# A residual batch of per-sample matrix products: one small transfer more at the head of SyncE's queue, and another condition for the first store

## The chip, the core and the metric

The kernel runs on one core of a Trainium2 chip. A core has engines with instruction queues of their own: TensorE (PE, the matrix products), VectorE (DVE), ScalarE (ACT), GpSimd (POOL) and SyncE (SP). They agree with one another through semaphores: an instruction may wait until a semaphore has reached a number, and raise one when it is done. Transfers between the HBM and the on-chip memory (SBUF) are done by 16 DMA engines, which all queues share; an instruction on SyncE or ScalarE issues a transfer, and the transfer raises a semaphore by 16 once it has landed. Products land in PSUM, a memory of accumulators that VectorE reads.

The metric is the device time of one execution in microseconds. The profile shows one execution; its span reaches from the first to the last instruction and is a little shorter than the time.

## The reference

A batch of 128 samples, each a matrix of 128 channels by 1024 steps in float32. Each sample names one of 8 subjects, each subject has a 128 by 128 weight matrix, and the output is the sample plus the product with its subject's matrix.

```python
# x: (128, 128, 1024) f32; itok_B_0_7: (128,) int32 in 0..7; L0_cond_weights: (8, 128, 128) f32
w = weights[subjects]
out = jnp.einsum('bct,bcd->bdt', x, w)
x = x + out
```

Input and output are 67.1 MB each, so at least 134.2 MB cross between HBM and SBUF; the weights add 0.5 MB.

## The kernel before

**Tiles and slots.** The work is cut into `NT` = 32 units of `H * G` = 4 samples (2 MB). `x_all` holds 12 slots (`SLOTS`) of one unit each, side by side in SBUF; unit i uses slot i modulo 12. A unit has two halves (h = 0, 1) of two samples. The result of a unit is written over its input in the slot, and the store goes out from there.

**ScalarE issues the loads** (lines 200 to 204): 4 transfers of 512 KB for each unit, all in order. The first 12 units wait for nothing; from unit 12 on, the loads of a unit wait until the store of the unit 12 before, out of the same slot, has landed (`emptied`). So 48 loads can be issued at once.

**GpSimd** (206 to 211) only waits for loads to land and tells TensorE, by `s_ready`.

**VectorE** first clears `zeros` and a piece of `index`, waits for the subject list (line 194, semaphore `s_given`), clamps and wraps it in three small steps (195 to 199), waits for the weights, and copies the matrices of the first four samples from `w_all` into `ws`. Then a loop over the units (226): for each half it waits for the products, adds PSUM and the slot's half in one instruction of 128 x 2048 elements (`add`, line 174, which raises `s_added` by 1), and copies the two weight matrices for the same half of the next unit (`place`, line 153).

**TensorE** runs three idle products on `zeros` and then a loop over the units (231): for each half it waits for the weights (`s_go`) and the data (`s_ready`) and makes four products of 512 columns.

**SyncE** has the subject list as its first transfer (line 180, one piece of 512 bytes, `s_given`), then the weights (line 181, 1,024 pieces of 512 bytes, `s_wall`). Then come the stores (213 to 218). Ahead of all of them it waits until the loads of slot 7 have landed (line 213, `AHEAD` = 8); after that, each store waits for its unit's two additions (line 217: `s_added` at 2i + 2 for unit i). A unit's store is one transfer of 2 MB; the last unit goes in smaller parts, and its last sample on line 238.

What stands ahead of line 213 on SyncE are the two small transfers; what stands behind it are the stores alone.

Of the kernel before, what the change touches and what calls it, by code (L numbers as in the profile page):

```python
# [30 lines left out]
G = 2  # L31
H = 2
# [4 lines left out]

P_SLOTS = 2

AHEAD = 8  # L40

DMA = 16

# [29 lines left out]
def kernel(  # L73
# [7 lines left out]
    nc = tc.nc  # L81
    B, C, T = x.shape
    S, _, D = weights.shape
    NT = B // (G * H)

    def sbuf(name, *shape, dtype=F32):
        return ctx.enter_context(nc.sbuf_tensor(name, list(shape), dtype)).ap()
# [10 lines left out]
    w_all = sbuf("w_all", C, S, D)  # L98
    ws = [sbuf(f"w{i}", C, 1, D) for i in range(H * G)]
    zeros = sbuf("zeros", C, N)  # L100
    given, near, wrap = (sbuf(name, 1, B, dtype=I32) for name in ("given", "near", "wrap"))
    index = sbuf("index", 1, B + H * G, dtype=I32)
    ps = [
# [3 lines left out]
    s_given = tc.alloc_semaphore("s_given")  # L107
# [4 lines left out]
    s_added = tc.alloc_semaphore("s_added")  # L112
# [4 lines left out]
    s_slot = [tc.alloc_semaphore(f"s_slot{k}") for k in range(SLOTS)]  # L117
    s_head = tc.alloc_semaphore("s_head")

    def emptied(i):  # L120
        turns = i // SLOTS
        return DMA * (H * G + 1) * turns - (DMA * G if i >= SLOTS and i % SLOTS == 0 else 0)

    def load(engine, i, q):
        transfer(
            nc,
            engine,
            xs[i % SLOTS][:, q, :],
            x[i * H * G + q].rearrange("(a r) t -> a (r t)", r=ROWS),
        ).then_inc(s_head if i * H * G + q < G else s_slot[i % SLOTS], DMA)  # L130

    def store(i, q0, q1):
        b = i * H * G
        transfer(
            nc,
            nc.sync,
            out[b + q0 : b + q1].rearrange("g d t -> d g t"),
            xs[i % SLOTS][:, q0:q1, :].rearrange("d (o g) t -> d o (g t)", g=min(G, q1 - q0)),
        ).then_inc(s_slot[i % SLOTS], DMA)

    def subjects_of(i):
        _, subject = nc.values_load_multi_w_load_instructions(
            index[0:1, i] if isinstance(i, slice) else index[0:1, bass.ds(i * (H * G), H * G)],
            engines=[mybir.EngineType.DVE],
            min_val=0,
            max_val=S - 1,
            skip_runtime_bounds_check_because="the index is clamped on the chip above",
        )
        return subject

    def place(h, subject):
        for q in range(h * G, (h + 1) * G):
            copy = nc.vector.tensor_copy(ws[q], w_all[:, bass.ds(subject[q], 1), :])  # L153
        copy.then_inc(s_go, 1)

    def multiply(slot, h):
        nc.tensor.wait_ge(s_go, 1).then_inc(s_go, -1)
        nc.tensor.wait_ge(s_ready, 1).then_inc(s_ready, -1)  # L158
        for q in range(h * G, (h + 1) * G):
            for t in range(0, T, N):  # L160
                at = slot * (H * G * T) + (q * T + t)
                mm = nc.tensor.matmul(  # L162
                    ps[h][:, q % G, t : t + N],
                    ws[q][:, 0, :],
                    x_all[:, bass.ds(at, N)],
                    start=True,
                    stop=True,
                )
        mm.then_inc(s_product, 1)

    def add(slot, h):
        mine = x_all[:, bass.ds(slot * (H * G * T) + h * G * T, G * T)]
        nc.vector.wait_ge(s_product, 1).then_inc(s_product, -1)  # L173
        nc.vector.tensor_tensor(  # L174
            mine, ps[h].rearrange("d g t -> d (g t)"), mine, ALU.add
        ).then_inc(s_added, 1)

    with tc.tile_critical():  # L178

        nc.sync.dma_start(given, subjects.rearrange("(o b) -> o b", o=1)).then_inc(s_given, DMA)  # L180
        nc.sync.dma_start(w_all, weights.rearrange("s c d -> c s d")).then_inc(s_wall, DMA)

        nc.vector.memset(zeros, 0.0).then_inc(s_zeros, 1)  # L183
        nc.tensor.wait_ge(s_zeros, 1)
        for _ in range(IDLE):
            nc.tensor.matmul(  # L186
                ps[P_SLOTS - 1][:, G - 1, :N], zeros[:, :D], zeros, start=True, stop=True
            )

        nc.vector.memset(index[:, B:], 0).then_inc(s_index, 1)  # L193
        nc.vector.wait_ge(s_given, DMA)
        nc.vector.tensor_scalar(near, given, -S, S - 1, ALU.max, ALU.min).then_inc(s_index, 1)  # L195
        nc.vector.wait_ge(s_index, 2)
        nc.vector.tensor_scalar(wrap, near, 0, S, ALU.is_lt, ALU.mult).then_inc(s_index, 1)  # L197
        nc.vector.wait_ge(s_index, 3)
        nc.vector.tensor_tensor(index[:, :B], near, wrap, ALU.add).then_inc(s_index, 1)  # L199
        for i in range(NT):  # L200
            if i >= SLOTS:
                nc.scalar.wait_ge(s_slot[i % SLOTS], emptied(i))
            for q in range(H * G):
                load(nc.scalar, i, q)

        for i in range(NT):
            if i == 0:
                nc.gpsimd.wait_ge(s_head, DMA * G).then_inc(s_ready, 1)
                nc.gpsimd.wait_ge(s_slot[0], DMA * G).then_inc(s_ready, 1)
            else:  # L210
                nc.gpsimd.wait_ge(s_slot[i % SLOTS], emptied(i) + DMA * H * G).then_inc(s_ready, H)

        nc.sync.wait_ge(s_slot[AHEAD - 1], DMA * H * G)
        for i in range(NT):
            for h in range(H):
                if i == NT - 1 or h == H - 1:
                    nc.sync.wait_ge(s_added, i * H + h + 1)
                    store(i, h * G if i == NT - 1 else 0, (h + 1) * G - (i * H + h == NT * H - 1))


        nc.vector.wait_ge(s_index, 4)
        nc.vector.wait_ge(s_wall, DMA)
        subject = subjects_of(slice(0, H * G))
        for h in range(H):
            place(h, subject)
        with nc.vector.Fori(0, NT) as turn:  # L226
            subject = subjects_of(turn + 1)
            for h in range(H):
                add(turn % SLOTS, h)
                place(h, subject)  # L230
        with nc.tensor.Fori(0, NT) as turn:
            for h in range(H):
                multiply(turn % SLOTS, h)
# [39 lines left out]
```

## Time and profile before

| | |
|---|---|
| time, median of 3 runs | 323.64 us (323.44 to 323.72) |
| time of the profiled execution | 323.44 us |
| its span | 321.7 us |
| TensorE products busy | 244.1 us (76%) |
| VectorE busy | 165.7 us (52%) |
| bytes read from HBM, written to it | 67.63 MB, 67.11 MB |
| SyncE's queue (q1), share of the 16 DMA engines | 50.1% |
| ScalarE's queue (q10), share of the 16 DMA engines | 49.6% |
| loads: 128 of 512 KB, median from issue to landing | 10.7 us |
| 2 MB stores: 31, median from issue to landing | 54.8 us |
| weights: issue to landing | 5.1 us |

How to read the profile: the page cuts the span into 40 equal slices and gives each engine's busy share in tenths (9 is 90% or more). The row DMA is the mean busy share of the 16 DMA engines, and below it stands what they moved in GB/s. A transfer is cut into packets that the engines work off one by one; a share over 1 in a short stretch comes of packets that overlap or reach past it. In a timeline a line gives start, length, engine, source line, operation and tiles; "SPq" and "ACTq" are the issuing queues of SyncE and ScalarE, and "x48" merges 48 instructions. L59 is the line in the helper `transfer` where all loads and stores are made, so loads and stores are told apart by their tiles and queues.

### The profile page before, as it was taken

The page shows a single profiled execution, that of the slowest core. Times are in us where ns is not written, and L with a number is a line of the kernel's source. Part 1 is how long each engine was busy: PE and PEld are TensorE (multiplying, and loading weights), DVE is VectorE, ACT ScalarE, POOL GpSimd, SP SyncE. Part 2 cuts the span into 40 slices and gives each one's busy share as a digit, 9 for nine tenths or more (in the row PEclk, how much of TensorE's full clock was granted, in tenths as well). Part 3 has the DMA queues.
Part 4 walks back from the last instruction along what each step waited for, and adds up shares of the span by engine and source line. Part 5 has one row for each costly group of instructions (what it writes and reads, how often), then busy time and mean ns, then how long its engine had stood idle before and what let it go on. Part 6 is the DMA issues. An engine that isn't in the chain of part 4 may idle for free. (4 is left out here: it accounts for less than half of the span.)

```text
span 321.7 us, 2380 instructions
## 1 busy us (share of the span) xinstructions
PE 244.1 (76%) x518; PEld 101.0 (31%) x518; DVE 165.7 (52%) x202; POOL 0.2 (0%) x4
## 2 busy tenths in 40 slices
PE   5999999999999999959499684986959779300000
PEld 2434444443444444424143231432423234000000
DVE  2267776777677677736627465371754707500000
POOL 0000000000000000000000000000000000000000
PEclk9799999999999999979879999897998959755555
DMA  7999999999999999999999999999999999999997
GB/s 281 426 428 426 424 424 408 421 437 418 421 438 428 422 418 426 439 427 423 424 418 425 434 435 413 426 433 427 428 418 425 440 417 421 426 430 425 427 428 309
DMA packets 16051, 134.76 MB, mean 419 GB/s; under 512 B 2609, under 2 KB 3634, under 8 KB 3890
## 3 DMA queue, kind: packets, MB, share of 16 engines
q1 hardware_dynamic: 9906, 67.64, 50.1%
q10 hardware_dynamic: 6144, 67.12, 49.6%
q14 instruction: 1, 0.01, 0.0%
HBM read 67.63 MB, written 67.11 MB: 419 GB/s over the span
## 5 line engine op out<-in xcount | busy, mean ns | idle before, releaser
L162 PE MATMUL ps<-x_all,w 128*128 x512 | 239.6, 626 | 30.2 <-PEq L158 27.1
L174 DVE TENSOR_TENSOR x_all<-ps,x_all 128x2048 f32 x64 | 146.7, 2292 | 106.9 <-DVEq L173 106.9
L162 PEld LDWEIGHTS ps<-x_all,w 128*128 128x128 f32 x512 | 99.3, 199 | 170.5 <-issue 169.7
L153 DVE COPY w<-w_all 128x128 f32 x132 | 23.2, 219 | 4.3 <-DMA w_all<-in_L_cond_weights_dram 4.3
L186 PE MATMUL ps<-zeros 128*128 128x512 f32 x6 | 4.4, 897 | 1.7 <-DVE zeros L183 1.7
L186 PEld LDWEIGHTS ps<-zeros 128*128 128x128 f32 x6 | 1.7, 304 | 3.6 <-issue 1.9
L183 DVE MEMSET zeros<- 128x512 f32 x1 | 0.5, 485 | 1.0 <-SPq L178 1.0
L195 DVE TENSOR_SCALAR near<-given 1x128 int32<-1x128 int32 x1 | 0.2, 217 | 0.6 <-DMA given<-in_itok_B_dram 0.6
L199 DVE CUSTOM_DVE_ANT_0 index<-near,wrap 1x256 uint16<-1x256 uint16 x1 | 0.3, 280 | 0.0
L197 DVE TENSOR_SCALAR wrap<-near 1x128 int32<-1x128 int32 x1 | 0.2, 215 | 0.0
L260 POOL MEMSET const-bfloat16-1.0<- 128x1 bf16 x1 | 0.1, 101 | 0.0
L260 POOL MEMSET const-uint8-127<- 128x1 uint8 x1 | 0.1, 101 | 0.0
L260 POOL MEMSET const-float32-0.0<- 128x1 f32 x1 | 0.1, 98 | 0.2 <-issue 0.2
L260 POOL MEMSET const-float32-1.0<- 128x1 f32 x1 | 0.1, 98 | 0.0
L260 DVE BASE_LOAD x1 | 0.0, 21 | 0.1
L193 DVE MEMSET index<- 1x4 int32 x1 | 0.1, 62 | 0.0
## 6 DMA issues: line engine op xcount, KB each, us to landing
x_all<-in_x_dram ACTq DMA_DIRECT2D x128, 512.0 KB, 10.7
out_dram<-x_all SPq DMA_DIRECT2D x31, 2048.0 KB, 54.8
out_dram<-x_all SPq DMA_DIRECT2D x1, 1024.0 KB, 26.0
out_dram<-x_all SPq DMA_DIRECT2D x2, 512.0 KB, 21.0
w_all<-in_L_cond_weights_dram SPq DMA_DIRECT2D x1, 512.0 KB, 5.1
given<-in_itok_B_dram SPq DMA_DIRECT2D x1, 0.5 KB
```

The source lines that it names most:

```text
L153: copy = nc.vector.tensor_copy(ws[q], w_all[:, bass.ds(subject[q], 1), :])
L162: mm = nc.tensor.matmul(ps[h][:, q % G, t : t + N], ws[q][:, 0, :], x_all[:, bass.ds(at, N)], start=True, stop=True,)
L174: nc.vector.tensor_tensor(mine, ps[h].rearrange("d g t -> d (g t)"), mine, ALU.add).then_inc(s_added, 1)
L183: nc.vector.memset(zeros, 0.0).then_inc(s_zeros, 1)
L186: nc.tensor.matmul(ps[P_SLOTS - 1][:, G - 1, :N], zeros[:, :D], zeros, start=True, stop=True)
L193: nc.vector.memset(index[:, B:], 0).then_inc(s_index, 1)
L195: nc.vector.tensor_scalar(near, given, -S, S - 1, ALU.max, ALU.min).then_inc(s_index, 1)
L197: nc.vector.tensor_scalar(wrap, near, 0, S, ALU.is_lt, ALU.mult).then_inc(s_index, 1)
L199: nc.vector.tensor_tensor(index[:, :B], near, wrap, ALU.add).then_inc(s_index, 1)
L260: nc = _bacc.Bacc("TRN2", target_bir_lowering=False, num_devices=1)
```

## The change

`AHEAD` becomes 4, and the wait for slot 7's loads goes away. In its place the condition of the stores of units 0 to 3 is raised: each waits until both additions of unit 3 are done (`s_added` at 8). From unit 4 on the condition is the same as before. Besides, SyncE issues a transfer ahead of the subject list: 16 pieces of 512 bytes out of the first 16 channels of sample 0, into a new tile `opening` of 16 partitions that nothing reads. It raises the same semaphore as the subject list, so VectorE's first step waits for both (32 instead of 16).

```diff
-AHEAD = 8
+AHEAD = 4
...
+    opening = sbuf("opening", DMA, D)
...
+        nc.sync.dma_start(opening, x[0, :DMA, :D]).then_inc(s_given, DMA)
         nc.sync.dma_start(given, subjects.rearrange("(o b) -> o b", o=1)).then_inc(s_given, DMA)
         nc.sync.dma_start(w_all, weights.rearrange("s c d -> c s d")).then_inc(s_wall, DMA)
...
-        nc.vector.wait_ge(s_given, DMA)
+        nc.vector.wait_ge(s_given, DMA * 2)
...
-        nc.sync.wait_ge(s_slot[AHEAD - 1], DMA * H * G)
         for i in range(NT):
             for h in range(H):
                 if i == NT - 1 or h == H - 1:
-                    nc.sync.wait_ge(s_added, i * H + h + 1)
+                    nc.sync.wait_ge(s_added, max(i, AHEAD - 1) * H + h + 1)
                     store(i, h * G if i == NT - 1 else 0, (h + 1) * G - (i * H + h == NT * H - 1))
```

## The prediction

> **What bounds the kernel now.** I read the page first, for the busy tenths and the DMA rows, then the DMA share by stretches of the span, then the waits of SyncE's queue, and last the timelines of the issuing queues and of VectorE. From the page:
>
> ```profile
> span 321.7 us, 2380 instructions
> DMA  7999999999999999999999999999999999999997
> GB/s 281 426 428 426 424 424 408 421 437 418 421 438 428 422 418 426 439 427 423 424 418 425 434 435 413 426 433 427 428 418 425 440 417 421 426 430 425 427 428 309
> DMA packets 16051, 134.76 MB, mean 419 GB/s; under 512 B 2609, under 2 KB 3634, under 8 KB 3890
> ```
>
> The DMA engines are full in 38 of 40 slices. No compute engine is: TensorE and VectorE stop for good in slice 34, long before the end. The bytes are fixed, so the time is the bytes at the full rate, plus what is lost where the rate falls. The view by stretches shows where that is; its columns are microseconds, the length, each engine's busy time, granted clock, DMA share and GB/s:
>
> ```profile
> 0.00:2.30 2.30, 0.64 (x1) 0.50 (x2) 0.59 (x4) 0.20 (x4) 1.00 0.22 50
> 2.30:6.30 4.00, 3.79 (x6) 1.20 (x4) 0.63 (x3) 0.00 (x0) 1.00 0.99 344
> 6.30:48.00 41.70, 39.70 (x87) 16.68 (x88) 26.10 (x34) 0.00 (x0) 0.96 1.01 428
> 48.00:51.00 3.00, 3.00 (x9) 1.32 (x8) 1.83 (x2) 0.00 (x0) 1.00 0.95 344
> 51.00:280.00 229.00, 196.94 (x420) 81.34 (x418) 136.57 (x162) 0.00 (x0) 0.94 1.01 426
> 280.00:319.20 39.20, 0.00 (x0) 0.00 (x0) 0.00 (x0) 0.00 (x0) 0.50 1.01 425
> 319.20:320.40 1.20, 0.00 (x0) 0.00 (x0) 0.00 (x0) 0.00 (x0) 0.50 0.31 126
> 320.40:321.70 1.30, 0.00 (x0) 0.00 (x0) 0.00 (x0) 0.00 (x0) 0.50 0.00 0
> ```
>
> Loads alone (6.3 to 48), loads and stores together (51 to 280) and stores alone (280 to 319.2) run at 428, 426 and 425 GB/s: the rate doesn't depend on the mixture. Length times rate over the rows comes back to 134.7 MB. What is lost against 426 GB/s is five pieces: 2.3 us before the first load; at the start 4.0 x (426 - 344) / 426 = 0.77 us; where the first store joins 3.0 x 82 / 426 = 0.58 us; at the end, where the sixteen engines don't finish together, 1.2 x (426 - 126) / 426 = 0.85 us; and 1.3 us after the last byte. The bytes at 426 GB/s are 316.3 us; with the five pieces that makes 322.1, 0.4 over the span, which is the rounding of rates. The profiled execution took 323.44 us, so 1.7 us lie around the span; it is 0.20 below the median of the three runs (323.64), and the sum below is made against it.
>
> **The change part by part.** It has two parts, one on SyncE's start and one on when the first store goes.
>
> *The wait of the first store.* The waits of SyncE's queue (what waited, for whom, total, times, longest):
>
> ```profile
> SPq L59 <- DMA x_all<-in_x_dram: 25.1, 1, 25.1
> SPq L217 <- DVE x_all L174: 17.9, 1, 17.9
> ```
>
> Its timeline (start, length, what), and VectorE's around 40 us:
>
> ```profile
> 0.95 0.35 SPq L180 DMA_DIRECT2D given<-in_itok_B_dram  x1
> 1.36 0.42 SPq L181 DMA_DIRECT2D w_all<-in_L_cond_weights_dram  x1
> 44.80 255.68 SPq L59 DMA_DIRECT2D out_dram<-x_all  x33
> 301.19 0.37 SPq L238 DMA_DIRECT2D out_dram<-x_all  x1
> ```
>
> ```profile
> 35.16 2.29 DVE L174 TENSOR_TENSOR x_all<-ps,x_all 128x2048 f32 x1 [1.12 <-DVEq L173]
> 38.52 2.29 DVE L174 TENSOR_TENSOR x_all<-ps,x_all 128x2048 f32 x1 [0.81 <-DVEq L173]
> 42.21 2.29 DVE L174 TENSOR_TENSOR x_all<-ps,x_all 128x2048 f32 x1 [1.12 <-DVEq L173]
> 45.57 2.29 DVE L174 TENSOR_TENSOR x_all<-ps,x_all 128x2048 f32 x1 [0.81 <-DVEq L173]
> ```
>
> The queue gets past slot 0's additions at about 1.8 + 17.9 = 19.7 and stands another 25.1 us, to 44.8, until slot 7's loads are in. After the change it stands until eight additions are done. Additions seven and eight are the rows at 35.16 and 38.52, so it is free at 38.52 + 2.29 = 40.8: the first store goes 4.0 us earlier. What is queued behind it on SyncE is stores alone. Those of slots 0 to 3 follow at once in both versions, since nine additions are done by 44.5; slot 4's needs ten, done at 47.9, in both.
>
> An earlier store takes turns on DMA engines that are full at that moment with loads. Every byte moved for a store between 41 and 45 is a byte of load moved later, and the rate is the same 426 to 428 either way. So the end moves only if the loads or the stores run dry somewhere. ScalarE's queue answers for the loads:
>
> ```profile
> 0.90 45.13 ACTq L59 DMA_DIRECT2D x_all<-in_x_dram  x48
> 61.95 0.48 ACTq L59 DMA_DIRECT2D x_all<-in_x_dram  x1
> ```
>
> The first 48 loads (25.2 MB) are issued by 46.0. Of these 50 + 4.0 x 344 + 41.7 x 428 kB, some 19 MB, are moved by 48 us, so 6 MB wait there: at half the rate 28 us of loads, to about 76. The 49th load, which needs slot 0's store, is issued at 61.95; with the change some 4 us sooner. The cover stays about 14 us, and after it the stores' backlog covers: from 280 on stores alone keep the engines full for 39 us, which shrinks by some 4 us at most. At the end the same bytes remain. The earlier start is worth 0. The 0.58 us lost where the first store joins moves from 48 to about 44; why it falls there the profile doesn't say, so I bound it: gone (-0.58) or paid twice (+0.58). I take 0, since a first store joins full load queues in both versions.
>
> *The opening transfer.* SyncE issues one more transfer, at the price of L180's row, 0.35 us, plus the 0.06 between L180 and L181: the subject list and the weights are issued 0.41 us later. Behind them wait VectorE's index arithmetic, the first weight copies and the first matmul:
>
> ```profile
> 2.22 0.22 DVE L195 TENSOR_SCALAR near<-given 1x128 int32<-1x128 int32 x1 [0.62 <-DMA given<-in_itok_B_dram]
> 7.31 0.63 DVE L153 COPY w<-w_all 128x128 f32 x4 [4.31 <-DMA w_all<-in_L_cond_weights_dram]
> 8.30 37.04 PE L162 MATMUL ps<-x_all,w 128*128 x80 [2.21 <-PEq L158]
> ```
>
> They come 0.41 us later, or 1.6 if the weights (524 kB) fall behind one more load of the same size, 1.2 us at 426 GB/s. Then the eighth addition ends between 41.2 and 42.4, still ahead of 44.8, and compute has its slack to the end: cost 0. Without the stores' backlog the 0.41 to 1.6 us would count in full. SyncE's wait for nothing else gets longer: the opening's semaphore, now 32, holds VectorE's first step alone, and the tile is read by nobody.
>
> On the DMA engines the opening is 16 packets, one each. Their price comes from the weights' pieces of the same 512 bytes, in the DMA view of the first 10 us (queue 1 is SyncE's):
>
> ```profile
> DMA packets 1262, 3.08 MB, mean 308 GB/s; under 512 B 81, under 2 KB 1106, under 8 KB 1106
> q10 hardware_dynamic: 220, 2.56, 64.3%
> q1 hardware_dynamic: 1042, 0.52, 17.6%
> ```
>
> 17.6% of 10 us is 1.76 us an engine for 64 pieces, so 0.03 us for one. That is the sure cost.
>
> What the trace doesn't show is what the opening does to the loss at the start. The stretches of 0.5 us there:
>
> ```profile
> 1.50:2.00 0.50, 0.34 (x1) 0.34 (x2) 0.10 (x2) 0.00 (x0) 1.00 0.00 1
> 2.00:2.50 0.50, 0.50 (x1) 0.16 (x1) 0.25 (x2) 0.00 (x0) 1.00 1.54 393
> 2.50:3.00 0.50, 0.50 (x2) 0.33 (x1) 0.47 (x2) 0.00 (x0) 1.00 0.40 131
> 3.00:3.50 0.50, 0.50 (x1) 0.01 (x1) 0.00 (x0) 0.00 (x0) 1.00 1.27 492
> ```
>
> The first packets of all engines begin together (share 1.54, counted where a packet starts) and then little new starts for half a microsecond: first packets run long. Of the 0.77 us lost, the weights' small pieces explain 1.76 - 0.524 / 0.426 = 0.53; the remaining 0.24 is the least that the cold engines cost, 0.77 the most. If the opening's packets wake the engines before the loads arrive, that much goes (-0.24 to -0.77); if they are served first and the loads' first packets run long all the same, as much may come on top (+0.77). I take 0: the loads are issued at 0.90, ahead of SyncE's first transfer at 0.95, and `given`, also 512 bytes and first in its queue, precedes them today on some engine without the start being whole.
>
> The Trainium skill speaks against such a transfer: "DMA: Bandwidth & Descriptors", section "Bandwidth", gives 0.68 us for a 4 KB transfer issued from GpSimd and calls anything under 64 KB mostly overhead. Held against the 0.03 us above, its 0.68 would make the sum 324.1 instead of 323.5; it holds only if the engines stand still for that time, and no run here shows the opening's 8 KB yet.
>
> The sum: 323.44 + 0 (earlier stores) + 0 (later weights) + 0.03 (16 packets) + 0 (start) = 323.47, say 323.5. The end can shift too: the 0.85 us of uneven finish may vanish or double as packets fall differently; I take 0 and keep a few tenths of it for the range.
>
> **The rivals.**
>
> *The opening wakes the engines.* The whole start loss goes: 323.47 - 0.77 = 322.7. For it: the first packets run long on all engines at once, and the opening touches all sixteen, where `given` is one piece. Against: 0.53 of the 0.77 has another explanation, and then only 323.2 remains, which can't be told from no change. From 0.65 us on it counts as faster.
>
> *The opening pushes the loads back.* The bound is a full set of DMA engines from 2.3 us on, so whatever delays the first load delays the end one for one. If the opening pays a cold start of its own ahead of the loads, 0.77 + 0.03 is added: 324.2. With only SyncE's 0.41 us of issue passed on it is 323.9, within the bound. For it: both queues feed the same engines within 0.1 us of each other. Against: the load is issued first.
>
> *Stores 4 us earlier end 4 us earlier.* 323.47 - 4.0 = 319.5. It would need idle DMA engines between 51 and 319; their share there is 1.01.
>
> *The finish becomes less even,* by another 0.85 us: 324.3. Nothing in the change aims at it; a shifted first store alters who waits for whom in 230 us of mixed traffic.
>
> **How the numbers follow.** A measurement of this kernel tells about 0.2%, 0.65 us, from no change. Forecast (no more than that either way) 0.55; woken engines 0.20, with another 0.03 for a finish that becomes more even; earlier end 0.03; loads pushed back 0.15; less even finish 0.04. That gives faster 0.26, same 0.55, slower 0.19. The range runs from the woken engines' 322.7 to the less even finish at 324.3, with 0.2 either side for the spread of the runs shown: 322.5 to 324.5. The forecast's own range is 323.0 to 324.0.
>
> **What would show it.** Right: first store issued at 41 to 42.5; the dip in the DMA rate at about 44 to 47 and as deep; 425 to 428 GB/s on either side; matmuls beginning at 8.7 to 9.9; the first loads' bytes still at 2.3. Wrong: a rate other than 426 in the mixed stretch, a first load stretch (2.3 to 6.3) clearly above or below 344 GB/s, first bytes after 2.6, or an engine idle after 51.

## The result, and the profile after

The changed kernel took 324.04 us (median of 22 runs, 323.68 to 328.49), the kernel before 323.50 (22 runs, 323.16 to 323.83) beside it: a ratio of 1.0033, 95% interval 1.0017 to 1.0049. It is slower by a third of a percent, where no difference was forecast. The 22 runs are of two kinds. Nineteen lie between 323.68 and 324.6, and their mean of 324.06 is 0.16% over the mean of before (323.53); three took 327.22, 328.24 and 328.49 us, and they make the other half of the 0.33%.

The profile is of an execution of 323.99 us, one of the nineteen. From its page, the lines that answer to those of before:

```profile
span 322.2 us, 2380 instructions
DMA  7999999999999999999999999999999999999996
GB/s 266 432 424 425 425 427 423 407 426 434 421 432 419 436 420 420 426 440 426 419 418 427 435 428 415 426 432 429 424 426 419 440 411 428 426 425 428 425 427 289
```

The DMA engines are as full as before. But the order of events at the start is another one. SyncE's timeline and rows of VectorE's (start, length, what, and the idle time ahead with what ended it):

```profile
0.96 0.39 SPq L182 DMA_DIRECT2D opening<-in_x_dram  x1
1.41 0.31 SPq L183 DMA_DIRECT2D given<-in_itok_B_dram  x1
1.76 0.41 SPq L184 DMA_DIRECT2D w_all<-in_L_cond_weights_dram  x1
55.40 245.31 SPq L59 DMA_DIRECT2D out_dram<-x_all  x33
```

```profile
20.60 0.63 DVE L154 COPY w<-w_all 128x128 f32 x4 [15.43 <-DMA w_all<-in_L_cond_weights_dram]
28.55 2.29 DVE L175 TENSOR_TENSOR x_all<-ps,x_all 128x2048 f32 x1 [7.31 <-DVEq L174]
...
49.72 2.29 DVE L175 TENSOR_TENSOR x_all<-ps,x_all 128x2048 f32 x1 [1.12 <-DVEq L174]
```

The weights are issued 0.40 us later than before (1.76 against 1.36) and land 13.3 us later: VectorE's copies begin at 20.60 instead of 7.31. The row at 49.72 is the seventh addition; the eighth, from 53.08 to 55.37, lets SyncE go, and the first store leaves at 55.40. That is 10.6 us later than before, not 4 earlier.

Where the weights' pieces went is seen in the DMA view by queue (packets, MB, share of the 16 engines); queue 1 is SyncE's. Before, from 2 to 6 us and from 6 to 20:

```profile
q1 hardware_dynamic: 1037, 0.52, 43.8%
...
q1 hardware_dynamic: 3, 0.00, 0.0%
```

After, the same two stretches:

```profile
q1 hardware_dynamic: 364, 0.18, 14.9%
...
q1 hardware_dynamic: 709, 0.35, 8.6%
```

Before, the 1,024 pieces of 512 bytes go in one burst ahead of the loads' next packets. After, two thirds of them are still to come at 6 us. Most of these 709 packets, 578, follow by 8 us; from 8 to 12, 12 to 16 and 16 to 20 us the queue still has

```profile
q1 hardware_dynamic: 67, 0.03, 2.8%
...
q1 hardware_dynamic: 46, 0.02, 1.8%
...
q1 hardware_dynamic: 18, 0.01, 0.7%
```

So there is still a burst, about 1.5 us later than before (half of the pieces have started by 4.8 us before and by 6.3 us after), and behind it a tail of 131 packets that stretches out among the loads' packets of 16 KB. The weights have landed only when the last piece has. The trace has sixteen steps in which their semaphore rises: before, all of them come between 5.8 and 6.5 us; after, nine come by 8.4 us and the other seven between 13.3 and 19.8.

The stretches of the span after (microseconds, length, engines, clock, DMA share, GB/s):

```profile
2.30:6.30 4.00, 4.00 (x6) 1.35 (x4) 0.71 (x3) 0.00 (x0) 1.00 0.90 301
6.30:58.00 51.70, 37.34 (x77) 15.28 (x77) 22.35 (x29) 0.00 (x0) 0.83 1.02 428
58.00:63.00 5.00, 5.00 (x13) 2.01 (x11) 3.89 (x6) 0.00 (x0) 1.00 1.00 401
63.00:280.00 217.00, 193.54 (x426) 80.40 (x424) 138.26 (x162) 0.00 (x0) 0.97 1.01 426
319.20:320.40 1.20, 0.00 (x0) 0.00 (x0) 0.00 (x0) 0.00 (x0) 0.50 0.45 181
320.40:320.90 0.50, 0.00 (x0) 0.00 (x0) 0.00 (x0) 0.00 (x0) 0.50 0.04 16
```

Against 426 GB/s the start loses 4.0 x 125 / 426 = 1.17 us (0.77 before), the first store's arrival 5.0 x 25 / 426 = 0.29 (0.58 before), and the finish, which now reaches to 320.9, 0.69 + 0.48 = 1.17 (0.85 before). The changes of +0.40, -0.29 and +0.32 add to 0.43 of the 0.5 us by which the span grew. The split is rough, since the row's end at 6.3 us falls into the late burst: over the first 20 us the DMA view counts 7.31 MB before and 7.23 MB after, which at 426 GB/s is 0.2 us and not 0.40. In this execution it is a matter of a few tenths at either end of the span, and the first store's 10 us cost nothing, since the loads filled the engines until then.

### The profile page after: what moved, and what is told of

Read it like the earlier page. It is cut to its first block, busy times and chain, and to the rows that moved or that the text cites. A ratio compares the mean times of both kernels' runs of the same rounds, so it can differ in the third digit from the quotient of the medians.

```text
span 322.2 us, 2380 instructions
## 1 busy us (share of the span) xinstructions
PE 240.5 (75%) x518; PEld 99.5 (31%) x518; DVE 165.7 (51%) x202; POOL 0.2 (0%) x4
## 5 line engine op out<-in xcount | busy, mean ns | idle before, releaser
L163 PE MATMUL ps<-x_all,w 128*128 x512 | 235.0, 617 | 33.3 <-PEq L159 19.0
L163 PEld LDWEIGHTS ps<-x_all,w 128*128 128x128 f32 x512 | 97.7, 196 | 171.4 <-issue 170.6
L189 PE MATMUL ps<-zeros 128*128 128x512 f32 x6 | 5.5, 1088 | 1.7 <-DVE zeros L186 1.7
```

Of the source, the lines that this page charges most:

```text
L163: mm = nc.tensor.matmul(ps[h][:, q % G, t : t + N], ws[q][:, 0, :], x_all[:, bass.ds(at, N)], start=True, stop=True,)
L189: nc.tensor.matmul(ps[P_SLOTS - 1][:, G - 1, :N], zeros[:, :D], zeros, start=True, stop=True)
```

## The experiments

Two theories went into them. **Theory W**: the weights miss their burst, drip in (come a piece at a time) among the loads, and everything follows from that. **Rival S**: the stores' new condition does it. **Rival C, later P**: the opening's sixteen packets cost by themselves. All ratios are to runs of the kernel before on the same chip, with 95% intervals. Diffs are against the changed kernel unless said otherwise.

**The parts alone.** First the opening with the old condition of the stores:

```diff
+        nc.sync.wait_ge(s_slot[AHEAD - 1], DMA * H * G)      # AHEAD = 8
-                    nc.sync.wait_ge(s_added, max(i, AHEAD - 1) * H + h + 1)
+                    nc.sync.wait_ge(s_added, i * H + h + 1)
```

> The opening transfer is kept, the stores' condition is the one of before (slot 7's loads, then each unit's own additions). Theory W (late weights): the opening makes the weights miss their burst between the first and second loads, so they land at about 20 us instead of 7 and the first matmul starts at about 21; the first store still goes at about 45, because slot 0's additions are done by 34. Time about 0.3 us over before from the start and the uneven finish, and no execution 4 us late. Rival S (the stores' condition alone does it): no difference to before, 323.5. Rival C (the sixteen packets themselves cost): weights land early, time as in the changed kernel, 324.0.

324.15 us, 1.0023 (1.0013 to 1.0034), highest of 11 runs 325.43. Weights landed 23.0 us after their issue, the first product at 26.50, the first store at 45.41. The price is there without the new condition; no run was 4 us late.

Then the condition alone:

```diff
-        nc.sync.dma_start(opening, x[0, :DMA, :D]).then_inc(s_given, DMA)
...
-        nc.vector.wait_ge(s_given, DMA * 2)
+        nc.vector.wait_ge(s_given, DMA)
```

> No opening transfer (its tile is still allocated, unwritten); the first stores wait for eight additions. Theory W: weights at 7.3 us, first store at 40.8, the dip of the DMA rate at about 45, time 323.5, within 0.2 us of before, no late execution. Rival S: 324.0, with some executions near 328, as in the changed kernel. Rival C: 323.5.

323.62 us, 1.0004 (0.9995 to 1.0013). Its SyncE timeline:

```profile
1.36 0.42 SPq L183 DMA_DIRECT2D w_all<-in_L_cond_weights_dram  x1
39.48 261.20 SPq L59 DMA_DIRECT2D out_dram<-x_all  x33
```

Here the first store does leave at about 40, 5 us sooner than before, and it is worth nothing that the runs resolve. Rival S, as the sole cause, falls.

**The place of the opening.** Issued third, behind the weights:

```diff
-        nc.sync.dma_start(opening, x[0, :DMA, :D]).then_inc(s_given, DMA)
         nc.sync.dma_start(given, ...).then_inc(s_given, DMA)
         nc.sync.dma_start(w_all, ...).then_inc(s_wall, DMA)
+        nc.sync.dma_start(opening, x[0, :DMA, :D]).then_inc(s_given, DMA)
```

> The changed kernel with the opening issued third, behind the subject list and the weights: the same sixteen packets and the same stores' condition. Theory W: the weights keep their place, land at about 7 us, first store at 40.8 to 41.5, time 323.5. Rival S: 324.0. Rival C: 324.0, since the packets are all still there.

323.58 us, 1.0004 (0.9995 to 1.0013), weights 4.9 us after their issue. The first store came at 43.88, later than expected: VectorE's first step waits for the opening too, which now lands behind the weights (7.52 us instead of 2.22), and the first product comes at 9.97. The same packets behind the weights cost nothing that the runs resolve.

With one piece instead of sixteen, ahead:

```diff
-        nc.sync.dma_start(opening, x[0, :DMA, :D]).then_inc(s_given, DMA)
+        nc.sync.dma_start(opening[:1], x[0, :1, :D]).then_inc(s_given, DMA)
```

> The changed kernel with an opening of one piece of 512 bytes in place of sixteen: the issue on SyncE stays, fifteen engines get no packet. Theory W, if it is the 0.4 us of issue that makes the weights miss their burst: as the changed kernel, weights at 15 to 20 us, first store at 50 to 56, 324.0. Theory W, if it is the packets that push them behind: weights at about 7 to 8 us, first store at 41, 323.5. Rival C: 323.5.

323.83 us, 1.0004 (0.9995 to 1.0013); the weights, issued at 1.64, landed after 8.9 us, the first store left at 45.46. Neither branch: half late, and within the noise.

The opening first, then the weights, the subject list last:

```diff
         nc.sync.dma_start(opening, ...).then_inc(s_given, DMA)
-        nc.sync.dma_start(given, ...).then_inc(s_given, DMA)
         nc.sync.dma_start(w_all, ...).then_inc(s_wall, DMA)
+        nc.sync.dma_start(given, ...).then_inc(s_given, DMA)
```

> The changed kernel with the subject list moved from second to third place: the opening is still first, but the weights are issued at 1.41 us, about as early as before (1.36). Theory W, if the time of issue decides: weights at about 7 us, first store near 41, 323.5 to 323.7. If the opening's packets alone, ahead in the same rings, make the weights miss their burst: weights at 15 us or later, 324.0. Rival P (the packets cost by themselves, some 0.4 us, wherever the weights are): weights early and yet 324.0.

Weights issued at 1.41 and landed after 4.9 us, first store at 41.75: with the sixteen packets ahead of them but issued in time, they make their burst. (The first product waits for the subject list here, until 9.50.) 323.85 us, 1.0008 (0.9999 to 1.0017): the median is 0.34 over before's (323.51), and the interval doesn't tell that from nothing.

**Lateness without an opening.** The weights held back until the first two samples are there, against the kernel with the new condition alone:

```diff
+        nc.sync.wait_ge(s_head, DMA * G)
         nc.sync.dma_start(w_all, ...).then_inc(s_wall, DMA)
```

> No opening; SyncE holds the weights back until the first two samples have landed (about 5 us), so that they meet full load queues on all engines; the stores keep the new condition. Theory W (a weight piece gets one turn for each 16 KB load packet once loads are queued): 64 turns of 0.62 us, weights at 35 to 48 us, first matmul just after, first store 34 us later at 70 to 83. By then the 48 loads (25.2 MB, done at about 62) have run dry: a hole of 8 to 20 us in the DMA rate, time 332 to 344. This is then also where single executions of the changed kernel near 328 can come from. Rival P (the opening's packets cost, not the lateness of the weights): weights late or not, no more than 324.

337.74 us, 1.0433 (1.0418 to 1.0449). SyncE's timeline and the stretches around the hole:

```profile
6.42 0.42 SPq L184 DMA_DIRECT2D w_all<-in_L_cond_weights_dram  x1
75.70 239.76 SPq L59 DMA_DIRECT2D out_dram<-x_all  x33
```

```profile
62.00:64.00 2.00, 2.00 (x6) 0.95 (x5) 1.04 (x1) 0.00 (x0) 1.00 0.97 410
64.00:68.00 4.00, 4.00 (x10) 1.61 (x9) 3.19 (x4) 0.00 (x0) 1.00 0.06 25
68.00:72.00 4.00, 4.00 (x10) 1.73 (x10) 2.88 (x4) 0.00 (x0) 1.00 0.00 0
72.00:76.00 4.00, 4.00 (x10) 1.63 (x9) 3.14 (x6) 0.00 (x0) 1.00 0.00 0
76.00:78.00 2.00, 2.00 (x6) 0.87 (x5) 0.93 (x1) 0.00 (x0) 1.00 0.48 197
```

From about 64 us all 12 slots are loaded, no store has gone, and the 16 DMA engines stand still until about 77, while TensorE and VectorE, which began at 41.89, work on the four units that the first store waits for. The weights landed at 40.1 us. While they came in, the queues took turns packet by packet: the DMA view counts 370 packets of each queue from 20 to 30 us. Theory W's 64 turns of 0.62 us, some 40 us, come out shorter, 33.7, since every third packet of the loads' queue is small: from 14 to 36 us the trace has 816 pieces of 512 bytes, 544 load packets of 16 KB and 272 of 4 bytes.

With the old condition the same lateness has no hole:

> The same held-back weights with the stores' condition of before. Theory W: weights at 35 to 48 us, first store after slot 0's additions, 10 us behind the first matmul, at 45 to 60, so no hole. What is left is the price of the late weights on the DMA engines: 323.8 to 324.5, the finish less even than before. Rival P: 323.5, since there is no opening.

Weights 33.9 us after their issue, first store at 53.60, 325.48 us, 1.0059 (1.0046 to 1.0072). More than expected, and the row of the loads' stretch says where part of it went:

```profile
6.30:44.00 37.70, 2.24 (x3) 1.18 (x4) 0.63 (x4) 0.00 (x0) 0.53 1.00 417
319.20:320.40 1.20, 0.00 (x0) 0.00 (x0) 0.00 (x0) 0.00 (x0) 0.50 0.79 321
```

417 instead of 428 GB/s (the changed kernel's row from 6.3 to 58) at a full DMA share, which is 37.7 x 11 / 428 = 1.0 us, and a finish that is nearly full where it was almost empty. So late weights cost DMA time by themselves, and with the new condition a hole on top.

**A small delay without a transfer.** Against the same kernel, SyncE waits for VectorE's clearing before it issues the weights:

```diff
+        nc.sync.wait_ge(s_index, 1)
         nc.sync.dma_start(w_all, ...).then_inc(s_wall, DMA)
```

> No opening at all; SyncE only waits for VectorE's clearing of its tiles (done at 1.6 us) before it issues the weights, which then go at about 1.7 us as in the changed kernel (1.76); the subject list stays at 0.95; the stores keep the new condition. Theory W (time of issue decides): weights at 10 to 21 us, first store at 45 to 56, 323.8 to 324.1. Rival P (the packets ahead in the rings do it): weights at 7 to 8 us, first store at 41, 323.5.

```profile
1.66 0.42 SPq L184 DMA_DIRECT2D w_all<-in_L_cond_weights_dram  x1
54.23 246.52 SPq L59 DMA_DIRECT2D out_dram<-x_all  x33
```

The weights, issued at 1.66, landed after 16.9 us; the first product came at 20.30, the first store at 54.23, nearly as in the changed kernel, with no opening in the queue. 323.82 us, 1.0005 (0.9995 to 1.0014). The same with the old condition:

> The same short delay with the stores' condition of before. Theory W: weights late in the same way, first store at about 45, 323.7 to 324.1 and no execution above 325.5. Rival P: 323.5.

Weights after 14.7 us, first store at 45.30; 323.86 us, 1.0011 (1.0000 to 1.0023). So 0.3 us of issue are enough to make the weights land 10 to 12 us later. The median is over before's (323.57) by 0.25 and 0.29 us, half of what the changed kernel shows.

**More of it.** Three openings of sixteen pieces instead of one, out of neighbouring columns of the same rows; VectorE's first step waits for all of them:

> The changed kernel with three openings of sixteen pieces in place of one: weights issued at about 2.6 us. Theory W: still later weights, at 25 to 40 us, first store 34 us behind them at 58 to 75, so most executions have a hole in the DMA rate, 326 to 337: the late executions of the changed kernel become the rule. Rival P: three times 0.5 us, 325.0, and no hole.

333.14 us, 1.0296 (1.0282 to 1.0310), all five runs between 331.77 and 333.38.

```profile
2.77 0.41 SPq L186 DMA_DIRECT2D w_all<-in_L_cond_weights_dram  x1
69.08 238.84 SPq L59 DMA_DIRECT2D out_dram<-x_all  x33
```

```profile
62.00:64.00 2.00, 2.00 (x6) 0.95 (x5) 0.88 (x4) 0.00 (x0) 1.00 0.80 336
64.00:66.00 2.00, 2.00 (x6) 0.76 (x4) 1.96 (x3) 0.00 (x0) 1.00 0.04 16
66.00:68.00 2.00, 2.00 (x6) 0.84 (x5) 1.23 (x1) 0.00 (x0) 1.00 0.00 0
68.00:70.00 2.00, 2.00 (x6) 0.80 (x6) 1.33 (x3) 0.00 (x0) 1.00 0.00 0
```

The hole again, 6 us shorter. Here the first store leaves 6.62 us sooner than in the kernel with the held-back weights (69.08 and 75.70), and the profiled executions are 6.68 us apart (331.77 and 338.45): past a point the end follows the first store one for one.

**The weights on ScalarE's queue,** ahead of the loads, with the new condition and no opening, and then with one opening and with three on SyncE:

```diff
-        nc.sync.dma_start(w_all, ...).then_inc(s_wall, DMA)
+        nc.scalar.dma_start(w_all, ...).then_inc(s_wall, DMA)
```

> No opening; the weights go first on ScalarE's queue, ahead of the loads, in the same rings as these; the stores keep the new condition. Both theories: weights at 4 to 5 us, the first load 0.5 us later, first store near 38, time 323.2 to 323.7. It is the control of the next run.

> The same with the opening first on SyncE, where it can't push the weights behind a load any more. Theory W: as the control, within 0.15 us, weights at 4 to 5 us. Rival P: 0.5 us over the control, as the opening's sixteen packets are all there.

> The weights first on ScalarE's queue, as in the control at 323.79, with three openings on SyncE. Theory W: weights at 4 to 5 us, and at most 0.3 us over the control. Rival P: three times the 0.46 us that one opening cost there, 325.2.

Weights after 3.9, 4.2 and 4.0 us, so never late. Times 323.79, 324.25 and 324.42 us; ratios 1.0009 (1.0000 to 1.0018), 1.0020 (1.0009 to 1.0030) and 1.0027 (1.0016 to 1.0038). Over the runs of the kernel before beside them (323.45, 323.45 and 323.51) that is 0.34, 0.80 and 0.91 us. Theory W had allowed 0.15 us over the control for one opening and 0.3 for three; 0.46 and 0.57 came out, while rival P's 1.4 for three did not. The intervals of neighbours overlap, but both kernels with openings lie clear of the kernel before, and their weights are never late. So theory W alone doesn't account for every cost: a few tenths seem to belong to an opening ahead of the loads' first packets, at least in this order of the queues, and they don't grow in proportion to its number. What makes them was not found.

**The weights first on SyncE,** against the kernel before:

```diff
+        nc.sync.dma_start(w_all, ...).then_inc(s_wall, DMA)
         nc.sync.dma_start(given, ...).then_inc(s_given, DMA)
-        nc.sync.dma_start(w_all, ...).then_inc(s_wall, DMA)
```

> The kernel before with the weights first on SyncE and the subject list second, no opening: weights issued at 0.95. Theory W: weights land before or among the first loads, at 4 to 6 us, nothing dripped; 323.2 to 323.5, the same as before or 0.1% better. Rival P: 323.5.

323.47 us, 0.9998 (0.9989 to 1.0007). No gain, and no version here beats the kernel before beyond its interval.

Set in order of the time at which SyncE issues the weights, the runs read (us; profiled execution for the first four columns, median for the last):

| kernel | weights issued | landed after | first product | first store | time |
|---|---|---|---|---|---|
| weights first, no opening, old condition | 0.95 | 5.4 | 8.07 | 44.47 | 323.47 |
| before | 1.36 | 5.1 | 8.30 | 44.80 | 323.50 |
| opening third | 1.36 | 4.9 | 9.97 | 43.88 | 323.58 |
| opening, weights, subjects | 1.41 | 4.9 | 9.50 | 41.75 | 323.85 |
| one piece | 1.64 | 8.9 | 12.28 | 45.46 | 323.83 |
| delay, old condition | 1.66 | 14.7 | 18.09 | 45.30 | 323.86 |
| delay, new condition | 1.66 | 16.9 | 20.30 | 54.23 | 323.82 |
| opening, old condition | 1.76 | 23.0 | 26.50 | 45.41 | 324.15 |
| the changed kernel | 1.76 | 18.0 | 21.51 | 55.40 | 324.04 |
| three openings | 2.77 | 32.2 | 36.72 | 69.08 | 333.14 |
| held back, old condition | 6.09 | 33.9 | 41.76 | 53.60 | 325.48 |
| held back, new condition | 6.42 | 33.7 | 41.89 | 75.70 | 337.74 |

Between 1.41 and 1.64 us lies the point from which on part of the weights' pieces is caught among the loads. The landing times are those of one execution each.

## Why the prediction was wrong

**The step that failed** is the later weights: "They come 0.41 us later, or 1.6 if the weights (524 kB) fall behind one more load of the same size, 1.2 us at 426 GB/s." The issue was late by 0.40 us as worked out, and for most of the pieces the 1.6 us came true: half of them had started 1.5 us later than before. But a transfer is done with its last piece, and the 1.2 us priced the weights as bytes in a queue that is drained in order, while the two queues take turns: in the held-back kernel the pieces go one at a time between the loads' packets (370 and 370 from 20 to 30 us), and in the changed kernel a tail of 131 packets came after 8 us. The weights landed 13.3 us later, and the first product came 13.2 us later. The next step fell with it: "compute has its slack to the end: cost 0" held for one wait, the old condition, which needs one unit's additions by 45 us. The new one needs four units', 7 us each, ahead of the first store, and so hands the lateness of compute to the stores. In the profiled execution this still cost nothing, as the loads filled the engines at 55.40; with weights later yet it makes the hole that begins at 64 us.

The prediction's own signs say the same: the first store at 55.40 (41 to 42.5 forecast), the dip in the rate at 58 to 63 (44 to 47), the first product at 21.51 (8.7 to 9.9) and a first load stretch of 301 GB/s (344). The rate of 425 to 428 GB/s and the time of the first bytes held. That 324.04 us still lies inside 322.5 to 324.5 is luck: the upper end was drawn from a less even finish, not from late weights. One slip in the sum of the span changes nothing in the forecast: of the 0.4 us left over, 2.3 x 50 / 426 = 0.27 are transfers in the first 2.3 us, which it counts as lost, and not the rounding of rates.

**The earlier first store** was right for the edit by itself (39.48 us, 1.0004) and wrong for the change, since the other part undid it. The cover worked out there assumed stores joining at about 44. Without any store the loads last until about 64, as the hole's rows show; at 55.40 some 8 us of that cover are left. Two parts that cost nothing alone were judged one by one; I didn't ask what the one does to the other's wait.

**The three late executions** were not foreseen. By the one-for-one rule of the two kernels with a hole, 328.49 us goes with a first store at about 75.70 - (338.45 - 328.49) = 65.7, ten microseconds later than in the profiled execution. Weights that drip in ten microseconds later would do it, and how late they land does change between runs: 18.0 us in the changed kernel's profile, 23.0 with the old condition. That the late executions have such a hole is inferred; none of them was profiled. With the old condition none of 11 was above 325.5, which three in 22 doesn't make impossible by chance; the delay with the new condition had none in 11 either (highest 324.14).

**The sixteen packets at 0.03 us** and **the start at 0** are not settled. Of the 0.5 us in ordinary executions, a delay without packets shows 0.25 to 0.29, and packets ahead of weights that are in time show 0.34, each with an interval that reaches or touches no difference. The two kernels with openings and the weights on ScalarE's queue are 0.80 and 0.91 us over the kernel before, clear of it, with no late weights at all, of which the control without an opening has 0.34. So late weights are shown to cost time where they are very late (325.48 us); what makes the 0.5 us of the changed kernel, the lateness or the opening itself, is open.

**The rivals.** Waking the engines: the start's rate was 301 GB/s, below 344, so no. Pushing the loads back: its time, 324.2, was near, but its mechanism was not there; the loads' first bytes came on time (507 GB/s from 2.0 to 2.5 us against 393). The less even finish came true in part, at 0.32 of its 0.85 us. The Trainium skill's 0.68 us for a 4 KB transfer issued from GpSimd ("DMA: Bandwidth & Descriptors", section "Bandwidth") was near in size, but the same opening behind the weights cost nothing that the runs resolve (1.0004, 0.9995 to 1.0013). The same page, section "Queues, rings and completion order", says that each DMA engine goes round between its queues packet by packet; the trace agrees for weights that meet full load queues (370 packets of each queue from 20 to 30 us in the held-back kernel), and the burst of before shows that many pieces can also pass in a row.

## What to carry to other kernels

Where two queues feed the same DMA engines, a small transfer of many pieces has to be issued before the other queue has filled; 0.3 us of issue decided here between landing after 5 us and after 15 to 17. Price a transfer that joins full queues by its number of pieces and turns, not by its bytes: 64 pieces for each engine took 33.7 to 33.9 us, where the bytes at 426 GB/s would take 1.2. And when a change has two parts, follow the delay of the one through the wait that the other introduces: a wait on finished work passes a late start on, a wait on loads doesn't.

## What was not expected of the hardware

1,024 pieces of 512 bytes took 33.9 us to land when issued into full load queues, and while they did, the DMA engines moved 417 instead of 428 GB/s with their share at 1.00. The pieces went one to each packet of the loads' queue, whether that was 16 KB or 4 bytes long. The landing time moved from 8.9 to 23.0 us among profiles of kernels that issued the weights within 0.12 us of each other (1.64 to 1.76).
